# Two of 32 row maxima of an attention step moved to ScalarE and GpSimd, and the small softmax steps to GpSimd

## The chip, the core and the metric

The kernel runs on one core of a Trainium2 chip. The metric is device time in microseconds (us) from one launch to its end; before the change it is 3719.4 us, the median of 3 runs (3716.38 to 3719.66). The core has five engines with a queue of instructions each: TensorE (PE in the profile; PEld is its weight load), VectorE (DVE), ScalarE (ACT), GpSimd (POOL) and SyncE (SP, which here only issues DMAs). They meet at semaphores. PSUM, where PE writes, is cut here into tiles of one bank (128 x 512 numbers) or a pair of banks.

## The reference, cut to what matters

Twelve layers follow each other on 2048 tokens of 128 numbers: four blocks of feed-forward, attention, feed-forward. The change touches three of the four attentions. The second one (the third adds a rotation of q and k, the first a causal mask and wider heads):

```python
x = x + _L0_attn_ref(_layernorm(x), ...)   # 8 heads of 16, causal
x = x + _L1_attn_ref(_layernorm(x), ...)   # 16 heads of 8
x = x + _L2_attn_ref(_layernorm(x), ...)   # 16 heads of 8
...
def _L1_attn_ref(x, w_qkv, w_proj, b_proj):
    ...
    attn = jnp.einsum('bnhd,bmhd->bhnm', q, k)
    attn = jax.nn.softmax(attn, axis=-1)
    out = jnp.einsum('bhnm,bmhd->bnhd', attn, v)
    out = out.reshape(B, N, C)
    return out @ w_proj.T + b_proj
```

In each head all 2048 tokens look at all 2048 tokens. The softmax subtracts each row's largest score before the exponential.

## The kernel before, in words

**Stages.** The twelve layers are stages named attn0, attn1, attn2 and so on. In the profile the attention steps of attn1 lie at about 791 to 1480 us and those of attn2 at about 1677 to 2387 us (first score tile to last exponential); both are without a mask. attn0 (about 178 to 450 us) is causal. All three go through `packed` (line 1325) and `flash` (line 974). attn3 uses `flash` too, with two heads at a time (`halved`).

**Iterations.** `packed` cuts the 16 heads of attn1 and attn2 into 4 groups of 4 heads and the 2048 queries into 4 chunks of 512: `its` has 16 iterations (line 1444), numbered n = 0 to 15. Two streams are woven together on PE:

- Stream A (`some`, line 1054) finds the row maxima of an iteration. For 4 tiles of 128 queries (`r`), 4 chunks of 512 keys (`kc`) and 2 pairs of heads (`j0`) PE writes 128 x 1024 scores into a pair of banks (line 1071) and DVE takes their maxima, two numbers per partition (line 1089): 32 such reductions for an iteration. The pairs of banks come from a pool with two of them (`banks`, line 76). The order of the 32 is `r` within two chunks: with (r, kc, j0), the pairs run (0,0,0), (0,0,2), (0,1,0), (0,1,2), (1,0,0) and so on; the chunks 2 and 3 follow.
- Stream B (`stream_b`, line 1127) makes the output of the iteration before. For each of 16 tiles of keys (`kt`) PE writes 4 transposed score tiles of 128 x 512 (line 1213, banks from a pool of three), ACT takes the exponential of each (line 1222) and PE multiplies by the values (line 1159).

**Between the two.** When the 32 reductions are done, `maxima` (line 1097) joins them and `put_max` (line 1551) splits the result into two bfloat16 numbers with two small DVE operations. Later `put` adds them to the queries (lines 1566 to 1574, tile `q2`), so that stream B can begin. At its end, `finish` (line 1579) copies the output to SBUF on ACT (`ov`, line 1582), PE turns it back (`po`, line 1587), and DVE takes the reciprocal of the row sums and multiplies by it (lines 1592, 1593). After the last group of heads `out_a` and `out_b` turn the result and multiply it by the output weights.

**What sets the order.** PE's instructions keep the order in which the program issues them (`tc.keep_in_program_order`). On the other engines a scheduler orders instructions at build time by a cost model of its own; the DVE reductions of stream A have `high_priority`. `after(delay, fn)` issues a step when a planner's clock has moved on by `delay`. Once built, each engine's list is fixed.

**The masked part.** In attn0 the diagonal chunk is masked on DVE: for each head one `tensor_tensor_reduce` adds a strip of the mask to the scores and takes the maximum (line 1081). attn3 masks on PE instead: `half_masks` (line 1021) adds the mask to the scores with four small matmuls for a pair of banks (line 1026).

Of the kernel before, what the change touches and what calls it, by code (L numbers as in the profile page):

```python
# [64 lines left out]
def tile_macaron(ctx: ExitStack, tc: tile.TileContext, a: dict, out: bass.AP, stages=STAGES):  # L65
# [31 lines left out]
    nc.gpsimd.memset(ones, 1.0)  # L97
    minus_half = const.tile([P, TC], F32, name="minus_half")
    nc.gpsimd.memset(minus_half, -0.5)

    def cs(name):
        return cst[:, slice(*CONSTS[name])]
# [864 lines left out]

    OUT_A = 4000.0

    def flash(io, pool, early, its, nh, causal, scale, s1, s2, pv_mm, put_max, begin, finish, poll=None,
# [7 lines left out]

        halved = nh == 2
        clock = [0.0]
        total = [0]
        later = []

# [7 lines left out]
        def after(delay, fn):  # L995
            later.append((clock[0] + delay, fn))
            later.sort(key=lambda v: v[0])
# [7 lines left out]
        def chunks(qc):  # L1005
            return qc + 1 if causal else NC

        if halved:

            halves = {}  # L1010
            for name in ("ident", "maskq", "maskk"):
                raw = pool().tile([P, 2, P], F32, name="halfraw", tag="halfraw", bufs=2)
                for j in range(2):
                    nc.sync.dma_start(
                        out=raw[P // 2 * j : P // 2 * (j + 1)],
                        in_=a["consts"][:, slice(*CONSTS[name])].rearrange("(b i) k -> i b k", b=2),
                    )
                halves[name] = pool().tile([P, 2, P], BF16, name="half" + name)
                nc.vector.tensor_copy(halves[name], raw)

        def half_masks(outs, mask):

            for b in range(2):
                for j in range(2):
# [1 line left out]
                    pe(nc.tensor.matmul(  # L1026
                        outs[j], halves["ident"][s, b], halves[mask][s, b], start=False, stop=b == 1
                    ))

        if tiled and causal:  # L1030
            junk = pool().tile([P, CH], F32, name="junk")
            strip = pool().tile([P, CH], F32, name="strip")
            nc.gpsimd.memset(strip[:, : CH - P], 0.0)
            nc.vector.tensor_copy(strip[:, CH - P :], cs("maskq"))

        ready = set()
        alive = [True]
# [16 lines left out]
        def some(n, turns, mp):  # L1054

            g, qc = its[n]
            nk = chunks(qc)
            for first, (r, kcs) in enumerate(turns):
                before = hook(n, kcs[0], r) if hook is not None else None
                if first == 0 and before is None:  # L1060
                    before = newest[0]
                for kc in kcs:
                    for j0 in range(0, nh, 2):
                        ps = first_pass_bank()
                        last = causal and kc == qc
                        masked = last and not tiled
                        w = (r + 1) * P if last else CH
                        for j in range(2):
                            o = j * CH
                            lhsT, rhs = s1(n, j0 + j, r, kc)  # L1070
                            pe(nc.tensor.matmul(  # L1071
                                ps[:, o : o + w], lhsT, rhs[:, :w], start=True, stop=not masked
                            ))
                            pos[0] += w
                        if masked:
                            half_masks([ps[:, j * CH + w - P : j * CH + w] for j in range(2)], "maskq")
                        both = ps.rearrange("p (j n) -> p j n", j=2)
                        with tc.high_priority() if not waiting[0] else nullcontext():
                            if last and tiled:
                                for j in range(2):  # L1080
                                    ins = nc.vector.tensor_tensor_reduce(
                                        junk[:, :w], both[:, j, :w], strip[:, CH - w :], 1.0, NEG,
                                        ALU.add, ALU.max, mp[:, r, j0 + j, kc : kc + 1],
                                    )
                                    if before is not None:
                                        in_order(ins, before)
                                        before = None
                            else:
                                ins = nc.vector.tensor_reduce(  # L1089
                                    mp[:, r, j0 : j0 + 2, kc], both[:, :, :w], AX.X, ALU.max,  # L1090
                                )
                        if before is not None:
                            in_order(ins, before)
                            before = None
                        yield 2 * w if tiled else w

        def maxima(n, mp):
            nk = chunks(its[n][1])
            mx = pool().tile([P, TC, nh], F32, name="mx", tag="mxa", bufs=3)
            nc.vector.tensor_reduce(mx, mp[:, :, :, :nk], AX.X, ALU.max, negate=True)  # L1100
            put, newest[0] = put_max(n, mx, pe)

            def done():
                put()
                ready.add(n)

            after(2000.0, done)

        newest = [None]
        waiting = [False]  # L1110
# [214 lines left out]
    def packed(io, early, hd, causal, scale, project, w, wv, wo, bias=None, outs=True):  # L1325
# [222 lines left out]
            o = (kt * 4 + j) * slot  # L1548
            return vt[its[n][0]][:, o : o + 32], slice(32 * j, 32 * j + 32)

        def put_max(n, mx, pe):
            top = tops[n % 3]
            tv = top.rearrange("p a r (j s) -> p a r j s", s=span)[:, :, :, :, 3:8:4]
            for i in range(nq):
                m = mx[:, :, i * per : (i + 1) * per]
                nc.vector.tensor_copy(tv[:, i, :, :, 0], m)
                last = nc.vector.tensor_tensor(
                    tv[:, i, :, :, 1], m, tv[:, i, :, :, 0], ALU.subtract
                )

            def put():

                t = room[0].tile([P, nq, CH], F32R, name="q2", tag="q2", bufs=3)
                for i in range(nq):
                    ps = bank("pm")
                    pe(nc.tensor.matmul(
                        ps, masks_b["ident_r"], qt[its[n]][:, i, :], start=True, stop=False
                    ))
                    for r in range(TC):
                        pe(nc.tensor.matmul(  # L1570
                            ps[:, r * P : (r + 1) * P], top[:, i, r, :], masks_b["ident_b"],
                            start=False, stop=r == TC - 1,
                        ))
                    nc.scalar.copy(t[:, i, :], ps)
                q2[its[n]] = t

            return put, last

        def finish(n, pv, after, pe):
            g, qc = its[n]  # L1580
            ov = room[1].tile([P, CH], F32, name="ov", tag="ov", bufs=2)
            nc.scalar.copy(ov, pv)  # L1582

            def normal():
                ps = bank("po")
                for r in range(TC):
                    pe(nc.tensor.transpose(
                        ps[:, r * P : (r + 1) * P], ov[:, r * P : (r + 1) * P], ident
                    ))
                po = ps.rearrange("p (r j m) -> p r j m", r=TC, j=4)  # L1590
                rc = room[0].tile([P, TC, 4], F32, name="rc", tag="rc", bufs=2)
                nc.vector.reciprocal(rc, po[:, :, :, hd])
                nc.vector.tensor_tensor(
                    os[qc][:, :, g * 4 * hd : (g + 1) * 4 * hd].rearrange(
                        "p r (j d) -> p r j d", j=4
                    ),
                    po[:, :, :, :hd],
                    rc.unsqueeze(3).to_broadcast([P, TC, 4, hd]),
                    ALU.mult,
                )  # L1600
                if g == n_groups - 1:
                    after(OUT_A if causal else 1500.0, out_a)

            def out_a():
                ps = bank("oT")
                for i in range(TC):
                    pe(nc.tensor.transpose(ps[:, i * P : (i + 1) * P], os[qc][:, i, :], ident))
                oT = room[1].tile([P, CH], F32, name="oT", tag="ov", bufs=2)
                nc.scalar.copy(oT, ps)
                after(1500.0, lambda: out_b(oT))  # L1610

            def out_b(oT):
                ps = bank("py").rearrange("p (i c) -> p i c", i=TC)
                for i in range(TC):
                    pe(nc.tensor.matmul(
                        ps[:, i, :], oT[:, i * P : (i + 1) * P], wo, start=True, stop=True
                    ))
                if bias is not None:
                    nc.gpsimd.tensor_tensor(xs[qc], xs[qc], over(bias, TC), ALU.add)
                nc.vector.tensor_tensor(xs[qc], xs[qc], ps, ALU.add)  # L1620
                io.mark(qc)

            after(1500.0, normal)
# [766 lines left out]
```

## Time and profile before

| what | value |
|---|---|
| median of 3 runs | 3719.4 us (3716.38 to 3719.66) |
| profiled execution, its own time | 3720.81 us |
| span of that execution, first to last instruction | 3719.1 us |
| mean granted TensorE clock | 0.950 of full speed |
| busy share of the span: PE, DVE, ACT, POOL | 92%, 77%, 54%, 22% |
| reductions of line 1089 | 1440, 1627.7 us busy |
| exponentials of line 1222 | 2368, 1220.5 us busy |

"Busy" of a group is the time in which at least one of its instructions ran, so it can be less than count times mean: consecutive instructions of one engine overlap by some tens of ns. The granted clock is given as a share of full speed. A timeline row gives start, length, engine, line and operation, output and input with their shapes, the number of merged instructions, and in brackets the idle time just before and what ended it. The tables of groups give count, busy us, mean ns, and the idle time before.

### The profile page before, as it was taken

Reading aid. Unit: us, or ns where it says so; the run is one execution under the profiler, and the core shown is the slowest. Engines: PE = TensorE matmul, PEld = TensorE weight load, DVE = VectorE, ACT = ScalarE, POOL = GpSimd, SP = SyncE. Lnnn points to the kernel's source line nnn. Section 1 sums busy time; section 2 is a strip of 40 time slices with the busy share of each in tenths; the row PEclk is TensorE's granted clock in tenths of the full one; section 3 lists DMA queues with packets and bytes.
Section 4 is the critical chain, followed back from the end, with each engine's and each line's share of the span. In section 5 each row is a group of like instructions: output and inputs, shape, how many; then the busy total and the mean of one; then the engine's idle time right before and its main releaser. Section 6 shows DMA issues by size and latency. Waiting matters only on the chain. (4 is left out here: it accounts for less than half of the span.)

```text
span 3719.1 us, 64518 instructions
## 1 busy us (share of the span) xinstructions
PE 3404.5 (92%) x25325; PEld 1837.3 (49%) x25325; DVE 2853.9 (77%) x4729; ACT 2025.6 (54%) x3815; POOL 817.1 (22%) x816
## 2 busy tenths in 40 slices
PE   7689987989999999997999999898889999999989
PEld 5543366854333333883333333376444444445457
DVE  6588556778999995778999999544777877788852
ACT  3346722317888888333888888731333344444442
POOL 1511124000000000210000000232555445533341
PEclk9779989979999999996999999898999999999999
DMA  3420123000000000100000000012443232211010
GB/s 106 98 52 14 37 62 91 7 20 9 15 6 16 6 4 7 55 25 21 10 16 10 12 6 1 26 44 68 151 146 112 96 106 98 97 57 52 24 35 12
DMA packets 124977, 170.18 MB, mean 46 GB/s; under 512 B 25152, under 2 KB 52930, under 8 KB 124672
## 3 DMA queue, kind: packets, MB, share of 16 engines
q1 hardware_dynamic: 122112, 160.80, 13.8%
q0 software_dynamic: 2560, 5.25, 0.9%
q8 instruction: 199, 3.26, 0.4%
q14 instruction: 106, 0.87, 0.1%
HBM read 101.25 MB, written 45.87 MB: 40 GB/s over the span
## 5 line engine op out<-in xcount | busy, mean ns | idle before, releaser
L1089 DVE TENSOR_REDUCE mp<-s 128x2 f32<-128x1024 f32 (+3 forms) x1440 | 1627.7, 1183 | 80.2 <-PE s L1071 56.7
L1222 ACT ACTIVATE pt<-s 128x512 f32<-128x512 f32 (+1 forms) x2368 | 1220.5, 601 | 217.7 <-PE s L1213 165.2
L1213 PE MATMUL s<-q,km 32*128 32x512 f32 (+2 forms) x2368 | 735.0, 493 | 28.8 <-ACT pt L1222 18.6
L1159 PE MATMUL pv<-pt,v 128*32 128x256 f32 (+1 forms) x8568 | 732.2, 414 | 22.9 <-ACT ov L1582 11.2
L1071 PE MATMUL s<-km,qt 32*128 32x512 f32 (+3 forms) x2368 | 617.1, 506 | 64.9 <-DVE mp L1089 45.3
L1213 PEld LDWEIGHTS s<-q,km 32*128 32x128 f32 (+1 forms) x2368 | 323.9, 184 | 531.4 <-issue 339.5
L1202 ACT ACTIVATE pt<-s 128x512 f32<-128x512 f32 (+3 forms) x640 | 306.3, 530 | 361.3 <-PE s L1194 216.3
L143 POOL TENSOR_TENSOR rs<-rs,minus_half 128x4 f32<-128x4 f32 x56 | 57.3, 1023 | 1491.8 <-DVE rs L142 1468.1
L2071 DVE TENSOR_TENSOR sum<-sum,pt 128x512 f32<-128x512 f32 (+3 forms) x328 | 260.0, 808 | 86.9 <-ACT pt L1202 85.6
L1159 PEld LDWEIGHTS pv<-pt,v 128*32 128x32 f32 x8568 | 169.2, 108 | 317.7 <-issue 147.1
L1194 PE MATMUL s<-q,k 64*128 64x512 f32 (+3 forms) x1920 | 295.1, 400 | 14.9 <-ACT pt L1202 10.5
L1159 PE MATMUL pv<-pt,latv 128*64 128x512 f32 (+3 forms) x1280 | 307.5, 560 | 1.3 <-ACT pt L1202 1.3
L2071 POOL TENSOR_TENSOR sum<-sum,pt 128x512 f32<-128x512 f32 (+1 forms) x200 | 264.7, 1324 | 179.8 <-ACT pt L1202 176.4
L1071 PEld LDWEIGHTS s<-km,qt 32*128 32x128 f32 (+1 forms) x2368 | 236.2, 191 | 123.8 <-DVE mp L1089 82.3
L1194 PEld LDWEIGHTS s<-q,k 64*128 64x128 f32 x1920 | 159.1, 186 | 222.8 <-issue 140.5
L715 ACT ACTIVATE sg<-pg 128x1024 f32<-128x1024 f32 x72 | 74.0, 1027 | 158.2 <-PE pg L229 142.0
L1071 PE MATMUL s<-k,q 64*128 64x512 f32 (+3 forms) x640 | 131.9, 430 | 19.0 <-DVE mp L1089 18.8
L1873 DVE TENSOR_TENSOR rot<-rot,tab 128x512 f32<-128x512 f32 x128 | 87.8, 686 | 74.8 <-PE rot L229 43.3
L725 PEld LDWEIGHTS pd<-l1d,h 128*128 128x128 f32 x1152 | 139.0, 191 | 5.6
L725 PE MATMUL pd<-l1d,h 128*128 128x128 f32 x1152 | 139.8, 275 | 0.0
L717 DVE TENSOR_TENSOR h<-pu,sg 128x1024 f32<-128x1024 f32 x72 | 87.8, 1220 | 51.7 <-PE pu L229 46.5
L1888 ACT CAST h<-rot 128x512 fp32r<-128x512 f32 x64 | 39.6, 619 | 159.5 <-POOL rot L1883 159.5
(572 smaller groups left out, 4736.3 us busy)
## 6 DMA issues: line engine op xcount, KB each, us to landing
tab<-in_l3rope SPq DMA_DIRECT2D x66, 256.0 KB
q<-q SPq DMA_DIRECT2D x32, 512.0 KB
k<-k SPq DMA_DIRECT2D x32, 512.0 KB
l0e<-in_l0e SPq DMA_DIRECT2D x32, 256.0 KB
q<-h SPq DMA_DIRECT2D x32, 256.0 KB
q<-rot SPq DMA_DIRECT2D x32, 256.0 KB
k<-h SPq DMA_DIRECT2D x32, 256.0 KB
k<-rot SPq DMA_DIRECT2D x32, 256.0 KB
```

What stands on the lines that cost most here:

```text
L715: nc.scalar.activation(sg, pg, AF.Silu)
L717: nc.vector.tensor_tensor(h.rearrange("p m n -> p (m n)"), pu, sg, ALU.mult)
L725: nc.tensor.matmul(pd[:, i, :], h[:, m, i * P : (i + 1) * P], wd[:, m, :], start=m == 0, stop=m == 1,)
L1071: pe(nc.tensor.matmul(ps[:, o : o + w], lhsT, rhs[:, :w], start=True, stop=not masked))
L1089: ins = nc.vector.tensor_reduce(mp[:, r, j0 : j0 + 2, kc], both[:, :, :w], AX.X, ALU.max,)
L1159: i = pe(nc.tensor.matmul(pv[out_rows, lo:hi], lhsT, pts[j][:, lo:hi], start=kt == 0, stop=kt == nt - 1 and hi == CH))
L1194: pe(nc.tensor.matmul(outs[j][:, c0:], lhsT, rhs[:, c0:], start=i == 0, stop=i == len(terms[0]) - 1 and not diag,))
L1202: ex = nc.scalar.activation(pts[j][:, c0:], outs[j][:, c0:], AF.Exp, scale=scale)
L1213: pe(nc.tensor.matmul(ps[:, c0:], lhsT, rhs[:, c0:], start=i == 0, stop=i == len(terms) - 1 and (tiled or not diag),))
L1222: ex = nc.scalar.activation(pt[:, c0:], ps[:, c0:], AF.Exp, scale=scale)
L1873: nc.vector.tensor_tensor(t.bitcast(F32), ps, halves["tabs"][i], ALU.mult)
L2071: eng.tensor_tensor(t[:, c0:], other[:, c0:], pts[j][:, c0:], ALU.add)
```

## The change

1. **Maxima aside.** In attn1 and attn2, for n from 1 to 15, two of the 32 reductions are done in another way: those of (r, kc, j0) = (1,0,0) and (1,2,2), pairs 4 and 21 when counted from 0. ACT copies the two banks to SBUF (two copies of 128 x 512). GpSimd halves the 512 keys three times, to 256, 128 and 64. A halving takes three operations: d = a - b, d = max(d, 0), a = d + b. DVE reduces the 64 that remain for each of the two heads. These instructions have no `high_priority`. The tiles `copied` and `over` have one buffer each.
2. **The two small operations of `put_max`** go to GpSimd for n from 1 to 15 in attn1 and attn2, and `put` is issued after a delay of 3000 instead of 2000.
3. **The end of an iteration.** For n from 0 to 14 in attn1 and attn2 ACT copies `po` to SBUF, and GpSimd takes the reciprocal as a power of -1 (128 x 16) and multiplies (128 x 128). For the last iteration, and in attn0, DVE does it as before.
4. **attn0's mask** moves to PE: `half_masks`, and then one DVE reduction for a pair of heads in place of two `tensor_tensor_reduce`. Four small DMAs and two DVE copies fetch what `half_masks` reads.

```diff
+    ASIDE = ((1, 0, 0), (1, 2, 2))
...
+        aside = tiled and not causal
...
-        if halved:
+        if causal:
...
-                        masked = last and not tiled
+                        masked = last
...
+                        if aside and n and (r, kc, j0) in ASIDE:
+                            halving(ps, mp[:, r, j0 : j0 + 2, kc])
+                            yield 2 * w
+                            continue
...
+        def halving(ps, out):
+
+            t = pool().tile([P, 2, CH], F32, name="copied", tag="copied", bufs=1)
+            d = pool().tile([P, 2, CH // 2], F32, name="over", tag="over", bufs=1)
+            for j in range(2):
+                nc.scalar.copy(t[:, j], ps[:, j * CH : (j + 1) * CH])
+            m = CH // 2
+            while m >= CH // 8:
+                nc.gpsimd.tensor_tensor(d[:, :, :m], t[:, :, :m], t[:, :, m : 2 * m], ALU.subtract)
+                nc.gpsimd.tensor_scalar_max(d[:, :, :m], d[:, :, :m], 0.0)
+                nc.gpsimd.tensor_tensor(t[:, :, :m], d[:, :, :m], t[:, :, m : 2 * m], ALU.add)
+                m //= 2
+            nc.vector.tensor_reduce(out, t[:, :, : 2 * m], AX.X, ALU.max)
...
-            put, newest[0] = put_max(n, mx, pe)
+            newest[0] = nc.vector.tensor_reduce(mx, mp[:, :, :, :nk], AX.X, ALU.max, negate=True)
+            if aside and n:
+
+                put, _ = put_max(n, mx, pe, nc.gpsimd)
+            else:
+                put, newest[0] = put_max(n, mx, pe)
...
-            after(2000.0, done)
+            after(3000.0 if aside and n else 2000.0, done)
...
+                else:
+                    ot = room[1].tile([P, CH], F32, name="ot", tag="ov", bufs=2)
+                    nc.scalar.copy(ot, ps)
+                    po = ot.rearrange("p (r j m) -> p r j m", r=TC, j=4)
+                    rc = room[0].tile([P, TC, 4], F32, name="rc", tag="rc", bufs=2)
+                    nc.gpsimd.tensor_tensor(rc, po[:, :, :, hd], minus_one, ALU.pow)
+                    nc.gpsimd.tensor_tensor(
+                        out, po[:, :, :, :hd],
+                        rc.unsqueeze(3).to_broadcast([P, TC, 4, hd]), ALU.mult,
+                    )
```

## The prediction

> **What bounds the kernel now.** I read the page first, then busy time by stage, the groups of instructions of attn1, the order in time of its DVE, and GpSimd's groups. Two stretches show the steady part of attn1 and attn2 (stretch, its length, then busy us of PE, PEld, DVE, ACT, POOL with instruction counts, granted clock, DMA share, GB/s):
>
> ```profile
> 850.00:1350.00 500.00, 485.10 (x4882) 186.92 (x4875) 481.85 (x479) 436.65 (x843) 0.00 (x0) 1.00 0.04 10
> 1800.00:2300.00 500.00, 484.82 (x4875) 188.29 (x4879) 485.86 (x499) 436.41 (x842) 4.83 (x4) 1.00 0.04 9
> ```
>
> DVE works 96 to 97% of the time, ACT 87%, GpSimd almost never, at full clock. PE's 97% says little, since ends of matmuls are modelled. The groups of attn1's stretch (DVE's five main ones, ACT's main one) and its DVE in order of time:
>
> ```profile
> L1089 DVE TENSOR_REDUCE mp<-s 128x2 f32<-128x1024 f32 x407 | 468.1, 1220 | 9.0 <-PE s L1071 5.1 <-PE s L1213 3.6
> L1593 DVE TENSOR_TENSOR o<-po,rc 128x128 f32<-128x128 f32 x12 | 3.5, 291 | 0.4
> L1592 DVE RECIPROCAL rc<-po 128x16 f32<-128x16 f32 x12 | 3.1, 255 | 5.9 <-PE po L1587 5.9
> L1557 DVE TENSOR_TENSOR top<-mx,top 128x16 bf16<-128x16 f32 x12 | 2.8, 232 | 0.4
> L1556 DVE CAST top<-mx 128x16 bf16<-128x16 f32 x12 | 2.4, 204 | 0.4
> ...
> L1222 ACT ACTIVATE pt<-s 128x512 f32<-128x512 f32 x816 | 425.8, 601 | 58.1 <-PE s L1213 35.4 <-PE s L1071 13.7 <-PE pv L1159 6.3
> ```
>
> ```profile
> 1064.79 16.19 DVE L1089 TENSOR_REDUCE mp<-s 128x2 f32<-128x1024 f32 x14
> 1081.01 0.22 DVE L1100 TENSOR_REDUCE mx<-mp 128x16 f32<-128x64 f32 x1
> 1081.26 0.20 DVE L1556 CAST top<-mx 128x16 bf16<-128x16 f32 x1
> 1081.50 0.23 DVE L1557 TENSOR_TENSOR top<-mx,top 128x16 bf16<-128x16 f32 x1
> 1081.60 8.01 DVE L1089 TENSOR_REDUCE mp<-s 128x2 f32<-128x1024 f32 x7
> 1090.34 0.26 DVE L1592 RECIPROCAL rc<-po 128x16 f32<-128x16 f32 x1 [0.73 <-PE po L1587]
> ```
>
> Reductions stand back to back: 16.19 us for 14, so one each 1.15 us (the 1220 ns of one overlap the next). The joining reductions (line 1100) start at 925.98 and, ten iterations later, at 1313.15: 38.7 us an iteration, of which 32 x 1.15 = 36.8 are reductions. ACT, idle 13%, waits for scores. So DVE is the bound, and 30 of the 32 iterations here are touched (15 in each stage). PE runs its list in order and has two pairs of banks for DVE: when DVE stands still, PE, and behind it ACT, stop after at most two more pairs.
>
> **Part 1, the maxima aside.** DVE loses two reductions, 2 x 1.15 us, and gains two over 128 elements: about 0.22 us each, as line 1100 has for 64. Relief: 1.87 us an iteration.
>
> What decides is where that last small reduction stands. In the built program's list for DVE it stands, for 55 of the 60 cases, directly after only two big reductions issued behind the aside pair (2 cases have one, 3 have layer-norm work besides):
>
> ```
> TensorReduce mp<-s_9115      pair before
>                              (s_9131 is the aside pair: ACT)
> TensorReduce mp<-s_9160
> TensorReduce mp<-s_9179
> TensorReduce mp<-copied      waits for ACT and for GpSimd
> TensorReduce mp<-s_9205
> ```
>
> So DVE has 2.3 us of work, and then waits for GpSimd's nine operations. Their price, from GpSimd rows of other stages (128x512 and 128x384 two-input, one-input, and the power):
>
> ```profile
> L2071 POOL TENSOR_TENSOR sum<-sum,pt 128x512 f32<-128x512 f32 x168 | 230.7, 1373 | 137.6 <-ACT pt L1202 134.7
> L143 POOL TENSOR_TENSOR rs<-rs,minus_half 128x4 f32<-128x4 f32 x56 | 57.3, 1023 | 1491.8 <-DVE rs L142 1468.1
> L876 POOL TENSOR_SCALAR h<-f 128x512 fp32r<-128x512 f32 x64 | 45.4, 713 | 122.6 <-ACT f L912 65.6 <-DVE f L890 56.8
> L2071 POOL TENSOR_TENSOR sum<-sum,pt 128x384 f32<-128x384 f32 x32 | 34.0, 1064 | 42.2 <-ACT pt L1202 41.7
> ```
>
> By line 2071's own view the undisturbed medians are 1278 ns at 512 and about 992 at 384 (shortest): 2.23 ns an element and 134 ns. The three halvings have 512, 256 and 128 elements a partition: two-input 2 x (1.28 + 0.71 + 0.42) = 4.8 us; one-input 0.71 + 0.42 + 0.28 = 1.4 us, scaled likewise. Each waits for the one before, some 0.04 us by DVE's dependent steps at 1081: 0.35 us. The chain is 6.6 us.
>
> The Trainium skill has a rule for the change and one against its size. "Perfetto Trace Analysis", section Optimizing Scalar/DVE Operations: with VectorE saturated, moving work to ScalarE or even GpSimd may make sense. By that rule alone the sum is the relief: -1.87 us an iteration. "SBUF — State Buffer", section SBUF: two separate sides: VectorE and GpSimd lock a shared pair of ports against each other when VectorE has two SBUF inputs. Line 2071 shows it (up to 1841 ns, 1.44 times the median), and with it the chain would be 9 us; but here DVE reads PSUM or stands still, so I take 6.6 and keep 9 as the upper end. The lower end is 5.4, if dependent steps cost nothing and the small ones are a third cheaper.
>
> Time line of an aside pair, PE's write at 0: the exponential issued ahead and two copies (0.52 + 2 x 0.55 us pitch, ACT 0.5 to 0.9 late) end near 2.4; the chain ends at 9.0; the small reduction at 9.25. DVE began the pair before at -0.55. So 9.8 us for four pairs that took 4.6 before: 5.2 us lost each time. Nothing gives it back: PE then holds two pairs at most, and DVE runs at 1.15 us a pair as before. Two asides: +10.4 us an iteration. The copies' ACT time (4 x 0.55) lies in that standstill.
>
> **Parts 2 and 3.** DVE loses 0.255 + 0.291 + 0.204 + 0.232 us and 5.9/12 = 0.49 us of waiting for `po`: -1.47 us an iteration. GpSimd's two small operations for `top` are awaited by PE 3 pairs (3.4 us) later; the power row's 1.02 us for each would still fit: nothing. GpSimd's power (1.02 us by the nearest row; up to 4.1 if it goes by element) and multiplication (128 elements, 0.42) stand behind the first chain in GpSimd's list and delay only `out_a`, which PE meets in n = 12 to 14 after two more pairs: o is ready at 9.0 + 1.0 to 4.1 + 0.4, so PE comes 1 to 4 us late: 6 times 1.5, +9 us in all. The copy `ot` and what is left of the turnover's idle time (1.4 us of DVE idle an iteration, 0.49 counted) mostly fall into the first standstill: -0.5 us an iteration.
>
> **Part 4, attn0.** DVE had 32 x (0.688 + 0.554 + 0.424 + 0.287 + 4 x 0.083) = 73 us there, and gets 16 x (1.22 + 0.94 + 0.65 + 0.37) = 51. PE gets 64 groups of four mask matmuls. From attn3's line 1026, 77.95 us for 256 groups: 0.305 us, 19.5 us. DVE and PE are both about 85% busy there, so the ends are -20 and +20 us; PE waited 23.6 us for the operation that goes, so I take -4. The four DMAs stand between loads of `y` on SP: up to 2.4 us later, inside these ends.
>
> **Sum.** An iteration: +10.4 - 1.47 - 0.5 = +8.4 us; times 30, +252 us. Five asides with less to lose: -10. `out_a`: +9. attn0: -4. Together +247 us on the profiled 3720.8 us (span 3719.1), which is 1.4 us above the median: 3719.4 + 247 = 3966 us.
>
> **Rivals.** *The cover holds.* If the small reduction found its data ready, only the relief and ACT's load count: ACT's 33.8 us an iteration (87.3% of 38.7) plus five copies of 0.54 makes 36.5, DVE's 38.7 - 1.87 - 1.47 = 35.4; ACT bounds, -2.2 us, 30 times: 3719 - 66 = 3653 us, faster. This needs a chain that ends within the 2.3 us of work behind the aside; the sign turns where an aside loses 1 us, at a chain of about 2.4 us. Against it: the two-input rows alone make 4.8 us. For it: only that DVE's list might be followed otherwise; yet DVE stood still 0.73 us for `po` with reductions queued behind. 6%.
>
> *ACT's copies in a row.* Without GpSimd's delay, but with no buffering, each aside tile of keys takes ACT 2.07 + 1.08 = 3.15 us in place of 2.3: 2 x 0.85 - 1.47 = +0.2 us an iteration, 3719 + 7 = 3726 us. Same or slightly slower; 4%.
>
> *The chain is dearer.* Port locking, or strided halves and waits that cost more: at 9 us an aside loses 7.6, +144 us more: 4110 us. 12%.
>
> **How the numbers follow.** The likeliest case, 3966, has 78%; its own bounds (chain 5.4 to 7.7 us with +-1.15 us x 58, about 67 us, and attn0's +-20) are about 3890 to 4040. The range takes in part of the dear chain: 3880 to 4060. A measurement of this kernel can tell about 0.2% from no change. Faster by over 0.2%: 6%; within 0.2%: 2%; slower by over 0.2%: 92% (half of the 4% counts as no change).
>
> **What would show it.** After: idle time of DVE before the small reduction, ended by GpSimd, about 4.5 us each 60 times, some 270 us; the nine GpSimd operations 6.2 us busy; an iteration of 47 us in attn1; ACT and PE less busy there; attn0 within 20 us. I would be wrong if that idle time were under 1 us, or if a GpSimd two-input operation over 512 took well under 1.28 us.

## The result and the profile after

The changed kernel takes 4310.8 us (median of 6 runs, 4281.1 to 4356.5) where the kernel before took 3716.2 us on the same chip (6 runs, 3711.8 to 3719.7): 1.159 times as long, 95% interval 1.154 to 1.163, or 589 us more. The ratio leaves out the run of 4356.5 us, which was in a slower state than the others. The sign was predicted; the size was not: 3966 us, at most 4060, had been forecast. The profiled execution took 4294.2 us (span 4292.5 us, mean granted clock 0.852 where it was 0.950).

The whole loss lies in attn1 and attn2. From the first to the last exponential, attn1 takes 932.0 us (637.5 before) and attn2 951.6 us (649.5 before): 597 us more together, where the whole span grew by 573. attn0's exponentials end 10 us earlier than before. Two stretches of the kernel after, in the columns of the prediction's first view:

```profile
850.00:1350.00 500.00, 410.94 (x3212) 135.77 (x3212) 306.08 (x286) 315.88 (x599) 162.12 (x185) 0.73 0.03 8
1900.00:2400.00 500.00, 412.44 (x2846) 176.24 (x2844) 326.60 (x406) 260.97 (x485) 141.91 (x162) 0.72 0.05 13
```

DVE, 96% busy before, is 61% busy in attn1. And a column that the prediction read once and then left has changed: the granted clock fell from 1.00 to 0.73. The groups of the first stretch:

```profile
L1083 DVE TENSOR_REDUCE mp<-s 128x2 f32<-128x1024 f32 x251 | 300.6, 1223 | 87.3 <-PE s L1225 70.3 <-PE s L1071 16.9
L1234 ACT ACTIVATE pt<-s 128x512 f32<-128x512 f32 x539 | 290.5, 604 | 172.5 <-PE s L1225 163.2 <-PE s L1071 4.5 <-PE pv L1171 4.0
L1100 POOL TENSOR_SCALAR over<-over 128x512 f32<-128x512 f32 x17 | 25.3, 1487 | 1.5
L1615 POOL TENSOR_TENSOR rc<-ot,minus_one 128x16 f32<-128x16 f32 x8 | 23.5, 2932 | 0.0
L1101 POOL TENSOR_TENSOR copied<-over,copied 128x512 f32<-128x512 f32 x17 | 21.6, 1273 | 1.4
...
L1103 DVE TENSOR_REDUCE mp<-copied 128x2 f32<-128x128 f32 x17 | 4.9, 289 | 102.8 <-POOL copied L1101 102.8
```

Two kinds of idle time are new on DVE: 102.8 us before the small reductions (6.0 us each, ended by GpSimd), and 87.3 us before the big ones, ended by PE. The second kind had been 9.0 us. One aside in order of time, first on DVE, then on GpSimd:

```profile
1012.06 1.23 DVE L1083 TENSOR_REDUCE mp<-s 128x2 f32<-128x1024 f32 x1 [0.18 <-PE s L1071]
1019.46 0.29 DVE L1103 TENSOR_REDUCE mp<-copied 128x2 f32<-128x128 f32 x1 [6.17 <-POOL copied L1101]
1019.66 3.48 DVE L1083 TENSOR_REDUCE mp<-s 128x2 f32<-128x1024 f32 x3
1023.54 1.23 DVE L1083 TENSOR_REDUCE mp<-s 128x2 f32<-128x1024 f32 x1 [0.40 <-PE s L1225]
1025.28 1.23 DVE L1083 TENSOR_REDUCE mp<-s 128x2 f32<-128x1024 f32 x1 [0.51 <-PE s L1225]
```

```profile
1011.01 1.27 POOL L1099 TENSOR_TENSOR over<-copied 128x512 f32<-128x512 f32 x1 [8.19 <-ACT copied L1096]
1012.36 1.48 POOL L1100 TENSOR_SCALAR over<-over 128x512 f32<-128x512 f32 x1
1013.93 1.27 POOL L1101 TENSOR_TENSOR copied<-over,copied 128x512 f32<-128x512 f32 x1
...
1018.97 0.45 POOL L1101 TENSOR_TENSOR copied<-over,copied 128x128 f32<-128x128 f32 x1
1019.38 2.93 POOL L1615 TENSOR_TENSOR rc<-ot,minus_one 128x16 f32<-128x16 f32 x1
```

The nine operations run from 1011.01 to 1019.42, 8.4 us, and the small reduction starts 0.04 us later. After three reductions without a wait, DVE waits 0.4 to 0.5 us before each: it now runs at PE's pace, 1.74 us a pair. PE's own row shows the standstill, and the same stretch cut finely (columns as above) shows the clock:

```profile
1016.83 0.49 PE L1225 MATMUL s<-q,km 32*128 32x512 f32 x1
1020.93 0.79 PE L1071 MATMUL s<-km,qt 32*128 32x512 f32 x2 [3.61 <-DVE mp L1083]
```

```profile
1016.00:1018.00 2.00, 1.32 (x10) 0.34 (x9) 0.00 (x0) 1.77 (x4) 1.75 (x4) 1.00 0.00 0
1018.00:1020.00 2.00, 0.00 (x0) 0.00 (x0) 0.54 (x2) 0.01 (x1) 1.83 (x4) 0.50 0.00 0
1020.00:1022.00 2.00, 1.07 (x7) 0.49 (x11) 2.00 (x3) 0.20 (x1) 2.00 (x1) 0.50 0.00 0
...
1030.00:1034.00 4.00, 4.00 (x32) 1.15 (x32) 2.59 (x4) 2.24 (x5) 0.00 (x0) 0.50 0.02 4
1034.00:1036.00 2.00, 2.00 (x23) 0.54 (x19) 1.70 (x2) 1.50 (x3) 0.00 (x0) 0.74 0.00 0
1036.00:1040.00 4.00, 4.00 (x44) 1.57 (x47) 4.00 (x4) 3.66 (x8) 0.00 (x0) 1.00 0.12 32
```

PE stops near 1017.3 and starts again at 1020.93. The clock is 0.50 in the slice 1018 to 1020 already, and stays there until about 1035, some 14 us after the restart. At half clock the same matmul takes 0.79 us in place of 0.49.

### The profile page after: what moved, and what is told of

The parts are those of the page before. It is cut to its first block, busy times and chain, and to the rows that moved or that the text cites. A ratio compares the mean times of both kernels' runs of the same rounds, so it can differ in the third digit from the quotient of the medians.

```text
span 4292.5 us, 65618 instructions
## 1 busy us (share of the span) xinstructions
PE 3709.0 (86%) x25581; PEld 1887.1 (44%) x25581; DVE 2805.1 (65%) x4418; ACT 2118.2 (49%) x3965; POOL 1396.8 (33%) x1476
## 5 line engine op out<-in xcount | busy, mean ns | idle before, releaser
L1083 DVE TENSOR_REDUCE mp<-s 128x2 f32<-128x1024 f32 (+3 forms) x1444 | 1645.9, 1167 | 374.0 <-PE s L1225 245.1
L1234 ACT ACTIVATE pt<-s 128x512 f32<-128x512 f32 (+1 forms) x2368 | 1248.8, 604 | 661.2 <-PE s L1225 621.4
L1071 PE MATMUL s<-km,qt 32*128 32x512 f32 (+3 forms) x2368 | 738.8, 610 | 271.3 <-DVE mp L1083 268.2
L1171 PE MATMUL pv<-pt,v 128*32 128x256 f32 (+1 forms) x8568 | 915.6, 508 | 46.0 <-ACT pt L1234 30.7
L1225 PE MATMUL s<-q,km 32*128 32x512 f32 (+2 forms) x2368 | 850.0, 595 | 35.7 <-ACT pt L1234 22.2
L1071 PEld LDWEIGHTS s<-km,qt 32*128 32x128 f32 (+1 forms) x2368 | 278.9, 227 | 342.1 <-DVE mp L1083 329.4
L1099 POOL TENSOR_TENSOR over<-copied 128x512 f32<-128x512 f32 x180 | 147.4, 819 | 827.1 <-ACT copied L1096 818.2
L1100 POOL TENSOR_SCALAR over<-over 128x512 f32<-128x512 f32 x180 | 171.4, 952 | 15.6
L1101 POOL TENSOR_TENSOR copied<-over,copied 128x512 f32<-128x512 f32 x180 | 146.9, 816 | 14.5
L1902 POOL TENSOR_TENSOR rot<-rot,rot 128x512 f32<-128x512 f32 x64 | 90.0, 1407 | 159.2 <-DVE rot L1892 152.0
```

Of the source, the lines that this page charges most:

```text
L1071: pe(nc.tensor.matmul(ps[:, o : o + w], lhsT, rhs[:, :w], start=True, stop=not masked))
L1083: ins = nc.vector.tensor_reduce(mp[:, r, j0 : j0 + 2, kc], both[:, :, :w], AX.X, ALU.max,)
L1099: nc.gpsimd.tensor_tensor(d[:, :, :m], t[:, :, :m], t[:, :, m : 2 * m], ALU.subtract)
L1100: nc.gpsimd.tensor_scalar_max(d[:, :, :m], d[:, :, :m], 0.0)
L1101: nc.gpsimd.tensor_tensor(t[:, :, :m], d[:, :, :m], t[:, :, m : 2 * m], ALU.add)
L1171: i = pe(nc.tensor.matmul(pv[out_rows, lo:hi], lhsT, pts[j][:, lo:hi], start=kt == 0, stop=kt == nt - 1 and hi == CH))
```

## The experiments

Besides before and after, twelve kernels were run, each beside the kernel before on its own chip (whose medians there were 3719 to 3741 us), so they are compared by ratio. To read the loop, the same ten iterations of attn1 are taken from each trace: from the third joining reduction (`mx`) to the thirteenth. The median is over 24 iterations inside attn1 and attn2, without the first and the last two of each stage. The next column is the median of those among the 24 in which the granted clock was 1.00 throughout, with their number.

| kernel | ratio to before (95%) | ten iterations, us each | median iteration | at full clock | clock | DVE's wait for an aside |
|---|---|---|---|---|---|---|
| before | 1 | 38.7 | 38.6 | 38.6 (24) | 0.950 | - |
| after | 1.159 (1.154 to 1.163) | 58.9 | 59.9 | none | 0.852 | 5.9 |
| e1_no_aside | 1.004 (1.003 to 1.006) | 39.1 | 39.1 | 39.1 (24) | 0.947 | - |
| p2_division_back | 0.999 (0.998 to 1.000) | 39.0 | 38.9 | 38.9 (24) | 0.949 | - |
| e5_copies_only | 1.024 (1.022 to 1.026) | 41.2 | 40.9 | 40.8 (21) | 0.941 | (1.1, for ACT) |
| e2_join9 | 1.033 (1.026 to 1.040) | 40.8 | 40.6 | 40.5 (18) | 0.932 | 0 |
| e6_join6 | 1.045 (1.041 to 1.048) | 42.9 | 41.6 | 41.5 (15) | 0.931 | 0.55 |
| c_short | 1.082 (1.079 to 1.085) | 47.8 | 48.4 | none | 0.893 | 2.6 |
| e4_join4 | 1.105 (1.102 to 1.107) | 52.7 | 51.6 | none | 0.875 | 2.5 |
| e3_awake | 1.114 (1.111 to 1.116) | 52.2 | 50.2 | 50.1 (16) | 0.933 | 6.0 |
| d1_half_reduce | 0.988 (0.984 to 0.991) | 38.8 | 38.6 | 38.6 (23) | 0.954 | - |
| s1_before_shift | 1.010 (1.007 to 1.013) | 38.3 | 38.2 | 37.9 (20) | 0.936 | - |
| s2_e1_shift | 1.007 (1.004 to 1.009) | 38.2 | 38.1 | 38.0 (22) | 0.944 | - |
| s3_jx9_shift | 1.042 (1.038 to 1.046) | 41.1 | 41.2 | 39.2 (11) | 0.918 | 0 |

**1. Without part 1: e1_no_aside.** Parts 2 to 4 alone.

```diff
-    ASIDE = ((1, 0, 0), (1, 2, 2))
+    ASIDE = ()
```

> The change without its first part: no maxima aside; the small steps of the softmax by GpSimd, the end of an iteration by ScalarE and GpSimd, and attn0's mask on PE stay. Wait theory (the loss is DVE's wait for the GpSimd chain and what follows from it): DVE is relieved of about 1.5 to 2 us in each of 30 iterations, minus some 20 us because PE waits for o behind the power (2.93 us): about 3680 us, at all events not above 3716. Rival (the GpSimd steps of the other parts, the 2.93 us power above all, carry a large share of the loss): above 3800 us.

Ratio 1.004: nothing is gained by parts 2 to 4, against the expectation. DVE is 95% busy where it was 97.7% (the same ten iterations), and the iteration is 0.4 us longer, not 1.5 us shorter. So the loss belongs to part 1, and the relief of DVE that the prediction credited does not show.

**2. The small reduction later: e2_join9, e6_join6, e4_join4.** The same operations, with each small reduction put behind nine, six or four later big ones by edges of order alone (as built it stands behind two).

```diff
-                            halving(ps, mp[:, r, j0 : j0 + 2, kc])
+                            joins.append([JOIN, halving(ps, mp[:, r, j0 : j0 + 2, kc])])
...
+                        for join in joins:
+                            join[0] -= 1
+                        if joins and joins[0][0] <= 0:
+                            behind.append(joins.pop(0)[1]())
+                            in_order(behind[0], ins)
```

> The whole change, with the last small reduction of each aside pair bound behind nine later big reductions on DVE, so that the chain of 8.4 us is covered. Wait theory: DVE's idle time before it falls from 355 us to under 20, the granted clock in attn1 is back above 0.95, and the time is 3650 to 3720 us (ScalarE with 36.5 us an iteration would then bound). Rival (ScalarE's four copies an iteration and GpSimd's load cost of themselves): above 3760 us though nothing waits.

> As the kernel with the join behind nine reductions, but behind four (in the change as it is: two). DVE's wait should be 3.3 to 3.8 us in place of 5.6 to 6.2. If loss goes with the wait alone: 60 x 2.3 us less than the change, about 4170 us. If PE's clock falls only after a standstill of about 2 us or more: either still about 4130 to 4170 with a clock near 0.75, or, if PE's standstill is now too short, about 3810 us with a clock above 0.93.

> The whole change with each small reduction behind six later big ones (by edges of order alone, as in the runs behind four and nine). With four VectorE waited 2.7 us an aside, and each further reduction is 1.15 us or more, so the wait should be 0 to 0.6 us. If the clock falls only after standstills of TensorE of 1 us and more, it stays near 1: iteration 40.5 to 42.5, ratio 1.03 to 1.05. If any standstill of it brings half clock: iteration 46 and more, ratio over 1.07.

The rows of the small reduction behind nine, and behind six:

```profile
L1114 DVE TENSOR_REDUCE mp<-copied 128x2 f32<-128x128 f32 x60 | 16.6, 277 | 0.0
```

```profile
L1114 DVE TENSOR_REDUCE mp<-copied 128x2 f32<-128x128 f32 x60 | 17.0, 283 | 33.0 <-POOL copied L1112 33.0
```

Behind nine the wait is gone, and 12.6 of the 15.9 per cent of loss are gone with it. Yet it is still 3.3% slower than before, as only the expectation's rival had it: there is a price apart from the wait. Behind six, the iterations at full clock take 0.9 us more than behind nine, for two waits of 0.55 us. Behind four, the wait was shorter than expected (2.5 us) and the ratio of 1.105, some 4105 us, was between the expected cases. An iteration took 51.6 us, 11 us more than with no wait, though two waits are only 5 us; none of the 24 was at full clock.

**3. A busy PE during the wait: e3_awake.** The whole change, with 18 matmuls of 128 x 512 in PE's list at the place where it stands still; nobody reads what they write.

```diff
+                            since[0] += 1
+                            if since[0] == 5:
+                                idle = bank("awake")
+                                for _ in range(AWAKE):
+                                    pe(nc.tensor.matmul(
+                                        idle, masks_b["ident_b"], awake[0], start=True, stop=True
+                                    ))
```

> The whole change with its wait, and 18 matmuls of 128x512 bf16 without use (some 3.9 us at full clock) in PE's list where it stands still behind each aside pair; their result is read by nobody. Clock theory (about half of the loss is that PE's granted clock falls to 0.50 after each standstill and stays there for about 14 us): the clock in attn1 rises from 0.73 to above 0.93 and the time falls by 150 to 300 us, to 4010 to 4160. Rival (the loss is DVE's wait alone; the low clock lies beside it): 4290 to 4330 us, unchanged or longer.

Its stretch in attn1 and its small reduction:

```profile
850.00:1350.00 500.00, 461.57 (x3844) 177.55 (x3843) 324.86 (x317) 340.76 (x650) 175.24 (x203) 0.93 0.03 9
```

```profile
L1114 DVE TENSOR_REDUCE mp<-copied 128x2 f32<-128x128 f32 x60 | 17.3, 288 | 359.2 <-POOL copied L1112 359.2
```

DVE waits as long as in the kernel after (359 and 355 us in all), but the clock is 0.93 in place of 0.73 and the kernel 4.5 hundredths of before's time, 167 us, faster, with work added. The half clock that comes with the standstills is a cost of its own. As 0.93 is not 1.00, 167 us is rather a lower figure. Sixteen of its 24 iterations ran at full clock, three of them in a row:

```profile
1117.97:1268.30 150.33, 140.88 (x1268) 55.41 (x1264) 106.08 (x103) 111.55 (x214) 58.02 (x66) 1.00 0.03 9
```

That is 50.1 us an iteration with the whole wait in it, 9.6 us more than behind nine; the kernel after, without one iteration at full clock, takes 59.9.

**4. A shorter chain: c_short.** The three one-input operations are left out, so that a halving keeps one half of its columns and the maxima of the other half are left out.

```diff
-                nc.gpsimd.tensor_scalar_max(d[:, :, :m], d[:, :, :m], 0.0)
```

> The whole change without the three one-input maximum steps of GpSimd's chain (six operations instead of nine; d is then added unclipped, so that a step keeps one half of its columns and the maxima of the other half are left out). In the run of the change these three took 1.48 + 0.84 + 0.52 us and some 0.25 us of gaps, 3.1 of 8.4 us. If VectorE's wait is the length of this chain less two reductions, it falls from 5.9 to about 2.8 us an aside (170 us in all where the change has 355). The time: by waits alone the iteration would be 40.5 (as with the small reduction behind nine) plus 2 x 2.8 = 46 us, ratio 1.075; with TensorE at half clock for some 10 us after each standstill it is 48 to 52, ratio 1.09 to 1.12 (the run with the small reduction behind four, with 2.7 us of wait, took 51.2 an iteration).

```profile
L1102 DVE TENSOR_REDUCE mp<-copied 128x2 f32<-128x128 f32 x60 | 17.3, 289 | 157.0 <-POOL copied L1100 157.0
```

The wait falls from 5.9 to 2.6 us, about what the chain lost (3.1 us expected): the wait is the chain less two reductions. The time, 1.082, lies between the 1.075 that was expected from waits alone and the 1.09 with half clock; the clock in attn1's stretch is 0.87 (0.73 in the kernel after).

**5. ACT's copies without GpSimd: e5_copies_only.** DVE reduces the copied scores itself, at the same place.

```diff
-            while m >= CH // 8:
...
-            nc.vector.tensor_reduce(out, t[:, :, : 2 * m], AX.X, ALU.max)
+            nc.vector.tensor_reduce(out, t, AX.X, ALU.max)
```

> The whole change without GpSimd's chain: ScalarE's two copies stay, and VectorE reduces the copied 128x1024 itself, at the place in its list where the small reduction stands (same result). No wait for GpSimd is left, and GpSimd is idle in the loop but for the rounding and division. If the copies cost what they do because ScalarE stands in TensorE's chain: steady iteration 40 to 41 us as with the small reduction behind nine (40.5), ratio 1.02 to 1.04. If that cost came from GpSimd working beside (the memory side shared, or its late results): iteration 39, ratio 1.002 to 1.01.

Ratio 1.024, iteration 40.9 us, about as with the small reduction behind nine (40.6). Against e1_no_aside that is 2.0% or 73 us for 60 pairs of copies: 1.2 us a pair, where two copies take ACT 1.07 us. At full clock it is less: 1.8 us an iteration here, where DVE waits 1.1 us for each pair of copies, and 1.5 us behind nine, where it doesn't wait: 0.7 to 0.9 us a pair. ACT has 12% of idle time in the loop of before, and yet its copies cost most of their length. That this is because ACT stands in PE's chain, as was expected, this run does not show; see 7.

**6. Is DVE the bound at all: d1_half_reduce.** The kernel before, whose big reductions in attn0, attn1 and attn2 read only half the columns (where no mask lies): the maxima of the other half are left out.

```diff
+                                v = w // 2 if tiled else w
...
-                                    mp[:, r, j0 : j0 + 2, kc], both[:, :, :w], AX.X, ALU.max,
+                                    mp[:, r, j0 : j0 + 2, kc], both[:, :, :v], AX.X, ALU.max,
```

> The kernel before, with one edit: the 128x1024 reductions of attn1 and attn2 read only the first half of each key block's columns (the maxima of the other half of the columns are left out, so the maxima are partly wrong). It takes about half of VectorE's 1.15 us from every reduction and touches nothing else. Theory A (VectorE is the only bound of the two stages): the iteration falls from 38.7 us to ScalarE's 36.5 or lower, 30 iterations x 2.2 us = 66 us, ratio about 0.98 (3650 us where the kernel before takes 3716). Theory B (a second chain of the same length, scores - exponentials - values - next scores, TensorE to ScalarE and back, also takes 2.30 us a key tile): ratio 0.995 to 1.003, iteration 38.0 to 39 us, and TensorE's wait for pt grows where VectorE's wait for scores appears.

Ten iterations of the kernel before, and the same ten of this one:

```profile
926.00:1313.20 387.20, 377.52 (x3834) 145.85 (x3834) 378.13 (x379) 341.49 (x660) 0.00 (x0) 1.00 0.04 11
```

```profile
895.50:1283.10 387.60, 378.26 (x3838) 145.80 (x3835) 232.28 (x378) 341.31 (x661) 0.00 (x0) 1.00 0.04 11
```

DVE's work falls from 378 to 232 us, and the ten iterations take 387.6 us where they took 387.2. In the steady loop DVE is not what alone sets the length, though it is 97.7% busy: something else is as long. The expected ratio was missed all the same: the 1.2% come from elsewhere, most of it (26.6 us) before attn1's first joining reduction, 16 us of that in attn0, whose reductions the edit shortened too, which the expectation had overlooked.

**7. What else has that length: s1_before_shift, s2_e1_shift, s3_jx9_shift.** The idea tested: PE writes scores, ACT takes four exponentials, PE multiplies by the values before it writes the scores after next, and this circle too takes 2.30 us a key tile, as long as two reductions. The values are issued half a key tile later, on the kernel before, on e1_no_aside and on e2_join9.

```diff
-                        if tiled and alive[0]:
-                            if at_j % 2:
-                                values(at_j // 2)
+                        if tiled and pend_half[0] and at_j == 1 and n:
+                            values(1)
...
+                        elif tiled and alive[0]:
+                            if at_j == 3:
+                                values(0 if kt else None)
```

> The kernel before, with the values of a key tile issued one half step later in TensorE's list in attn1 and attn2 (its first half after the fourth exponential of the next tile instead of after the second, the second half with the second exponential of the tile after that); nothing is added. This opens the chain scores - exponentials - values - next scores, and leaves VectorE's work as it was. Theory A (VectorE the only bound): ratio 0.998 to 1.003. Theory B (two bounds of the same length): the same, 0.994 to 1.003, since VectorE's 38.7 us an iteration remains; TensorE's waits of 0.31 us for pt before the values go away.

> Parts 2 to 4 alone (no maxima by GpSimd, as in e1_no_aside) with the values one half step later as in s1_before_shift. Theory B: with the TensorE-ScalarE chain open, the 1.5 us an iteration that VectorE was relieved of now show: 30 x 1.5 = 45 us less than e1_no_aside, ratio to the kernel before 0.988 to 0.995. Theory A gives what e1_no_aside gave, ratio 1.004 (1.002 to 1.006).

> The whole change with the small reduction behind nine big ones (as e2_join9, which took 1.033 times the kernel before) and the values one half step later. Theory B: the 1.0 us of two copies no longer stands in the TensorE-ScalarE chain, and most of the 3.3% goes: ratio 0.99 to 1.012. If ScalarE's copies cost what they do because of something other than that chain (ScalarE's total, or its place ahead of exponentials that TensorE needs for scores), the ratio stays at 1.025 to 1.04.

None is faster by ratio than the kernel that it was made from, against what was expected of the last two; s1_before_shift, with 1.010, is slower than its expectation. An iteration of s1_before_shift at full clock, and 36 us of another:

```profile
1086.90:1124.80 37.90, 37.45 (x378) 15.34 (x378) 37.35 (x37) 35.15 (x67) 0.00 (x0) 1.00 0.03 6
...
1931.00:1967.00 36.00, 36.00 (x244) 10.48 (x244) 25.16 (x22) 21.99 (x41) 0.00 (x0) 0.50 0.00 1
```

At full clock the iteration is 37.9 us, 0.7 less than before, with the same work for DVE; on the lighter DVE of e1_no_aside it is 38.0 us, 1.1 less than there. So the place of the values holds the loop at 38.6, and DVE's work alone allows 37.9 or less. But opening the circle yields no more than that. What holds at 37.9 is not shown: PE is 98.8% busy there by its modelled ends, DVE 98.5%. And the shift brought stretches at half clock, which cost more than it gave: this one began after waits of PE of only 0.54 and 0.29 us.

An iteration at full clock of e1_no_aside, s2_e1_shift, e2_join9 and s3_jx9_shift, in this order:

```profile
2042.65:2081.67 39.02, 38.25 (x393) 14.70 (x385) 37.18 (x36) 34.62 (x68) 3.83 (x4) 1.00 0.09 22
1225.67:1263.63 37.96, 37.24 (x381) 15.03 (x380) 36.70 (x34) 35.70 (x68) 3.84 (x4) 1.00 0.03 7
1263.51:1304.04 40.53, 38.50 (x393) 14.71 (x385) 35.32 (x34) 36.38 (x72) 19.36 (x22) 1.00 0.03 7
1040.86:1080.06 39.20, 37.97 (x378) 14.89 (x377) 35.20 (x34) 36.90 (x72) 19.41 (x22) 1.00 0.02 6
```

s3_jx9_shift takes 39.2 us at full clock (40.5 in e2_join9). That is 1.3 us less, hardly more than the 1.1 us that the same shift takes off without copies (e1_no_aside to s2_e1_shift). So at most some 0.2 of the 1.5 us that the copies cost an iteration came from this circle; the cause of the rest stays open. The clock of s3_jx9_shift is lower too (0.918), and the total is no better. Why the clock falls more often with the values later stays open.

**8. Division back on DVE: p2_division_back.** e1_no_aside with the reciprocal and product of the kernel before.

```diff
-                if causal or n == len(its) - 1:
+                if True:
```

> Parts 2 and 4 alone: no maxima by GpSimd, and the division back on VectorE (reciprocal and product from PSUM, no copy by ScalarE, no power by GpSimd); GpSimd keeps the rounding of the maxima. Against e1_no_aside it takes the 128x512 copy out of ScalarE and the 2.9 us powers out of the way to the output. Theory: the 0.4 us an iteration and the tails of the two stages (iterations of 48.6, 47.1, 50.3 us where before has 44.4, 43.0, 45.0) go back to before's, steady iteration 38.5 to 38.6, ratio 0.996 to 1.002. Rival (the rounding by GpSimd, not the division, cost it): ratio stays 1.003 to 1.006.

Ratio 0.999: the 0.4% of e1_no_aside were the division. They are for the most part not in the steady loop (38.9 and 39.1 us), but at the ends of the stages. PE's waits there for the divided output, in e1_no_aside and in the kernel after (line waited at, releaser, us, times, longest):

```profile
PE oT L1626 <- POOL o L1616: 13.9, 6, 2.5
```

```profile
PE oT L1626 <- POOL o L1616: 31.5, 6, 6.6
```

No kernel here with the change's idea in it beats the kernel before; rounding by GpSimd and attn0's mask on PE together make no difference that these runs can tell.

## Why the prediction was right and wrong

The sign and the place of the loss were right, and at full clock the price of the wait comes out once its chain has its measured length. Two steps of the sum failed: the chain was sized at 6.6 us and took 8.4, and PE's clock after the standstills was put at nothing.

With 3716.2 us times the ratios, the loss of 589 us is the sum of three terms, against the 247 us of the prediction (its second term is what 247 leaves when the first, taken from a rival, is -66):

| term | predicted | measured | from |
|---|---|---|---|
| everything but the wait (the rival *the cover holds*) | -66 | +121 | e2_join9 |
| the wait for GpSimd (`out_a` and small terms with it) | +313 | +301 | e3_awake less e2_join9 |
| PE's clock after the standstills | not in the sum | +167 | after less e3_awake |

These are differences between whole kernels, and the first two are not free of the clock: over attn1 and attn2 it was 0.99 and 0.98 before, 0.96 and 0.92 in e2_join9, 0.93 and 0.94 in e3_awake, and 0.75 and 0.74 after. The iterations at full clock have no such share. There the whole change costs 50.1 - 38.6 = 11.5 us an iteration (e3_awake). The prediction's +8.4, with 2 x 1.8 us more for the chain as measured, is 12.0 us. That it comes so near is in part luck: its relief of DVE bought nothing where it could be measured, and something was given back that it left out.

- **The place of the wait: right.** The small reduction stands still 60 times, ended by GpSimd's last addition, PE and ACT stop behind it, and the kernel is slower.
- **The chain, 6.6 us: too short, the first step that failed.** Two-input steps took 1.27, 0.73 and 0.45 us, as estimated. The one-input steps, scaled from a row that writes another type (0.71 us), took 1.48, 0.84 and 0.52: 2.84 us in place of 1.4. A gap is 0.08 to 0.09 us, not 0.04. Sum 8.4 us; DVE idles 355 us in place of 270. By the prediction's own rule this is worth 1.8 us x 60, 109 us, and would have given 4075 us. So the rival *the chain is dearer* was right in its direction, though not in its cause; 233 us of the loss are still missing.
- **"At full clock": read, and not carried on; the larger step that failed.** The stretches of before show 1.00, and the prediction let PE stand still 60 times at no price but the time itself. The clock then falls to half, and PE needs 1.74 us a half step where DVE needs 1.15 until the clock comes back. That is 167 us, and rather more, since in e3_awake it still stood at 0.93. Of the 66 us that then remain, up to 22 are `out_a` (below); the rest is not taken apart.
- **"So DVE is the bound": a wrong reading.** The busy share showed that DVE had no room, not that nothing else had the same length. Halving its reductions leaves the iteration at 38.6 us. Hence, where nothing waits, the -1.47 and -1.87 us an iteration bought nothing (e1_no_aside, e2_join9). What the error did to the sum for the change itself is not shown: at full clock that sum comes out within 0.5 us.
- **"Nothing gives it back": not quite.** Two waits, 11.8 us together, cost 9.6 us an iteration at full clock (e3_awake less e2_join9), so about a fifth came back. Where is not shown.
- **"The copies' ACT time lies in that standstill": not shown either way.** Without a standstill the copies cost 1.5 us an iteration at full clock (e2_join9 less e1_no_aside), where the rival had ACT's free time take them. With it, they may be part of what came back. Over the whole kernel e2_join9 is another 33 us slower than e5_copies_only; about 24 us of that lie in the last two iterations of each stage (56.0, 52.5, 58.5 and 53.2 us where e5_copies_only has 50.1, 47.8, 51.3 and 47.3), where the power stands behind the chain on GpSimd and PE waits for `o` (31.5 us in place of 14.8). The remaining 9 us are less than the interval of e2_join9 can tell.
- **The power, 1.02 us "up to 4.1": inside its ends, but `out_a` was sized too small.** The power took 2.93 us for 16 numbers a partition. `out_a` waited 31.5 us on PE, not 9. The direction, and the place, were right.
- **The two rules of the Trainium skill.** "Perfetto Trace Analysis" lets work leave a saturated VectorE; here the relief alone bought nothing (e1_no_aside, ratio 1.004). The port lock of "SBUF — State Buffer" did not show in the chain: its two-input steps kept to 1.27 us. Nor is line 2071 clear evidence of it: its 38 instructions of 128 x 512 over 1.35 us all ran beside VectorE instructions with two SBUF inputs, but so did 98 of the 130 shorter ones.
- **attn0, -4 us: within its ends.** Its exponentials end 10 us earlier.
- **What would show it.** An iteration of 47 us was forecast and 59 came; nine operations of 6.2 us busy were forecast and took 7.7.

What stays open: the cause of most of the copies' price, and what brings the clock back.

## What to carry to other kernels

An engine that is 97% busy is the bound only if nothing else, a circle through other engines for one, has the same length: take half its work away and look at the steady iteration before you pay for relieving it. Idle time of another engine is not free room: here ACT was 12% idle, and copies of 2.1 us an iteration still cost 1.5. And a wait that stops PE costs the wait and then the half clock: 14 us at half clock are 8 pairs at 1.74 in place of 1.15 us, which by this estimate can lose 4.7 us, more than the standstill of 3.6 us itself. Put the joining operation as far behind the slow chain as its buffers allow.

## What was not expected of the hardware

- The clock went to 0.50 within 0.7 us of PE's stop (1017.3 to 1018.0) and stayed there for 14 us after a standstill of 3.61 us. In e4_join4 it was 13 us after 2.83 us (restart at 1044.72, full at about 1058) and 3 to 4 us after 1.33 us (restart at 1019.96, full from 1024); in s1_before_shift it was 41 us (1928 to 1969) after waits of 0.54 and 0.29 us (matmuls at 1924.52 and 1926.77).
- The length of one wait is not the measure. In the clock records of all fourteen traces the changes lie on a grid of 3.41 us. Of the steps of this grid at full clock in which PE, by its modelled ends, was busy for less than half of the step, 405 of 421 were followed by half clock; with PE busy for 90% or more, 2 of 10463 were. At half clock with PE busy below 70%, all 712 steps were followed by another one at half clock. With PE busy throughout, 519 of 1099 still were, so what brings the clock back is not found.
- GpSimd's maximum with a constant over 128 x 512 (f32 to f32) takes 1.48 us, longer than its subtraction of two inputs (1.27 us).
- GpSimd's power takes 1.01 us for 4 numbers a partition (exponent -0.5, line 145) and 2.93 us for 16 (exponent -1): 0.16 us for each further one, if the exponent makes no difference.
